# A selective scan on one core: ScalarE's products redistributed over a chunk, the product delta*x behind the matrix work, sums first in their place, finish and gate drawn out

## The chip, the cores and the metric

The kernel runs on one core of a Trainium2 chip. A core has five engines that run side by side, each with its own instruction stream: TensorE (PE in the profile, with its weight loads PEld), VectorE (DVE), ScalarE (ACT), GpSimd (POOL) and SyncE (SP, which here only issues DMAs). They wait for one another through semaphores. The metric is the time of one execution on the device, in microseconds (us); the kernel before takes 30205.28 us, the median of 3 runs (30204.43 to 30206.26).

## What is computed

Two layers work on an image of 256 x 256 tokens with 128 channels, all in float32. The first is row-wise attention with a pair bias and a gate. The second is a block with a two-dimensional selective scan: a projection to 256 inner channels, a depthwise 3x3 convolution and silu, then four scans (rows and columns, forwards and backwards), whose outputs are added, normalised, gated and projected back. The change touches only the scan stage. Its core in the reference:

```
delta = jax.nn.softplus(dts + dt_bias[None, :, :, None])
def step(h, inp):
    d_t, x_t, B_t, C_t = inp
    dA = jnp.exp(d_t[..., None] * As)
    h = dA * h + (d_t * x_t)[..., None] * B_t[:, :, None, :]
    y = jnp.einsum('bkdn,bkn->bkd', h, C_t)
    return (h, y)
```

So each of 256 channels has 16 states n. Per token the state is multiplied by exp(-delta*A), delta*x*B is added, and the output is the sum over n of h*C. After the four directions: y is normalised over its 256 channels, multiplied by the gate z = silu(...), multiplied by `w_out`, and added to the layer's input.

## The kernel before

The scan stage takes the last 24.5 ms of the span. It goes through 512 **chunks** q of 512 tokens: directions k in the order 2, 1, 3, 0, with 128 chunks each. A chunk has eight **steps** g, one for each group of 32 channels; on the 128 partitions lie 32 channels times 4 sets of states, and each partition holds 4 states i. A step has four places n = 0 to 3. I number the places of a chunk t = 4g + n, from 0 to 31; a number with a prime (1') is a place of the next chunk.

All instructions of the stage are recorded in the order of the program text (`manual_schedule`), so each engine executes exactly in the order in which the loop at L1140 to L1200 names its work. In every step:

- ACT makes four decays exp(delta*A): two go to the PSUM tile `dA`, of which there is one (places 0 and 1, L1109), and two to `dAl` in SBUF, two buffers, for the step after (places 2 and 3).
- DVE runs a scan of 512 on state 2 at place 0 and on state 3 at place 1 (L1176), each reading a `dAl` and a PSUM tile `bl`; at place 2 the product `bx<-B_r,ur` for the next step (L892, in `begin`); at place 3 one scan of 1024 over states 0 and 1 together, which reads `dA` (L1193).
- PE turns products back into `bl` (`turn_back`, L867) right after each short scan, and spreads delta*x over the partitions into the only `ur` tile (`spread_du`, L882) at place 2.
- POOL adds the carried state to the next step's first column (L1125), saves the last column times `a0x` (L1197), and multiplies the whole `bx` tile by C (L1200).

`bx` has 7 buffers: the product at place 2 of step g=6 writes the buffer that step g=0 of the same chunk had, and the one of g=2 the buffer of g=4 of the chunk before.

Around the steps, generators supply one piece of their work at each place, a piece ending at a `yield`; `until(a, b)` yields b - a times and so puts empty places in:

- `prepare(q+2)` readies a chunk two ahead: PE turns the tokens (`tps`), ACT copies them (`xs`, L752), PE projects (`pb`), ACT copies (`bc`), PE makes `pv`, ACT computes delta by Softplus (L776) and stores it by DMA; POOL multiplies delta*x (L781); PE turns `bc` and `xs` (`tpb`, `tpd`), ACT copies (`B_t` L790, `duT` L825). For the carry between chunks POOL forms `a0x` = A*delta of the first token (L813) and ACT takes its Exp (L821). The PSUM tag "mm" has 2 buffers for all these tiles.
- `products(q+1)` has 32 products duT*B on ACT (`bt`, L855), one a piece.
- `sums(q, h)` adds h*C over the states with PE, 16 matmuls in 4 pieces (`yp`, L906), half a chunk each.
- `store` (the first three directions) adds the partial output of an earlier direction to the new one on PE (`tpy`), ACT copies it (`yt`), a DMA stores it. `finish` (the last direction) adds in the same way (`ysum`), then normalises: ACT copies `ys` (L981), DVE takes statistics (L989, L991), POOL forms the inverse root (L36 to L994), ACT applies it (L997), PE turns (`tpz`), ACT scales (`gz`, L1021), POOL multiplies by the gate (L1025), PE projects (`po`, L1034), ACT copies (`xo`, L1044).

Within a place the order is: the place's decay, the pieces in a fixed order (`later`, which holds store and finish; preparing; replicating; multiplying; summing), then the scan or product of the place with its `turn_back` or `spread_du`.

Of the kernel before, what the change touches and what calls it, by code (L numbers as in the profile page):

```python
# [11 lines left out]
ALU = mybir.AluOpType  # L12
# [54 lines left out]
def attention_and_scan_kernel(  # L67
# [27 lines left out]
    nc = tc.nc  # L95
# [635 lines left out]
    def until(now, then):  # L731

        for _ in range(then - now):
            yield

    def prepare(q):

        k, a = steps[q]
        xt = loaded.pop(q)
        xs = io.tile([P, 2, T], F32, name="xs", bufs=3)  # L740
        tps = []
        for h in range(2):
            tp = sps.tile([P, T], F32, name="tps", tag="mm")
            for j in range(4):
                nc.tensor.transpose(  # L745
                    tp[:, j * P : (j + 1) * P], xt[:, j, h * P : (h + 1) * P], ident
                )
            tps.append(tp)
            yield
        yield from until(2, 4)  # L750
        for h, tp in enumerate(tps):
            nc.scalar.copy(xs[:, h, ::-1] if k >= 2 else xs[:, h, :], tp)  # L752
            yield
        yield from until(6, 7)
        pb = sps.tile([R + 2 * NS, T], F32, name="pb", tag="mm")
        for h in range(2):
            nc.tensor.matmul(
                pb, xw_in[:, k, h, :], xs[:, h, :], start=(h == 0), stop=(h == 1)
            )
        yield from until(7, 10)  # L760
        bc = io.tile([R + 2 * NS, T], F32, name="bc", bufs=1)
        nc.scalar.copy(bc, pb)
        bc_d = sd.tile([2 * NS, T], F32, name="bc_d")
        nc.sync.dma_start(bc_d, bc[R:, :])
        yield from until(10, 12)
        delta = io.tile([P, 2, T], F32, name="delta", tag="xd", bufs=1)
        pvs = []
        for h in range(2):
            pv = sps.tile([P, T], F32, name="pv", tag="mm")
            nc.tensor.matmul(  # L770
                pv, dtw_s[:, k, h * P : (h + 1) * P], bc[:R, :], start=True, stop=True
            )
            pvs.append(pv)
        yield from until(12, 15)
        for h, pv in enumerate(pvs):
            nc.scalar.activation(  # L776
                delta[:, h, :], pv, AF.Softplus, bias=dtb_s[:, k, h : h + 1]
            )
        de_d = sd.tile([DI, T], F32, name="de_d", bufs=3)
        nc.sync.dma_start(de_d.rearrange("(h p) t -> p h t", p=P), delta)  # L780
        nc.gpsimd.tensor_tensor(xs, delta, xs, ALU.mult)  # L781
        yield
        tp = sps.tile([P, 4, R + 2 * NS], F32, name="tpb", tag="mm")
        for b in range(4):
            nc.tensor.transpose(
                tp[:, b, :], bc[:, b * P : (b + 1) * P], ident[: R + 2 * NS, : R + 2 * NS]
            )
        yield from until(16, 18)
        B_t = io.tile([P, 4, R + 2 * NS], F32, name="B_t")
        nc.scalar.copy(B_t, tp)  # L790
        yield from until(18, 20)
        de0 = io.tile([P, NG, 1], F32, name="de0", bufs=1)
        if a:
            for j in range(4):
                nc.sync.dma_start(
                    de0[32 * j : 32 * j + 32],
                    de_d.rearrange("(g c) t -> c g t", c=32)[:, :, 0:1],
                )
        yield from until(20, 24)
        tps = []  # L800
        for w in range(2):
            tp = sps.tile([P, 2, DI], F32, name="tpd", tag="mm")
            for b in range(2):
                for h in range(2):
                    t0 = (2 * w + b) * P
                    nc.tensor.transpose(
                        tp[:, b, h * P : (h + 1) * P], xs[:, h, t0 : t0 + P], ident
                    )
            tps.append(tp)
            yield  # L810
        first = a0x[:, q % 2, :, :NB]
        if a:
            nc.gpsimd.tensor_tensor(  # L813
                first,
                A_s[:, k, :, :, :NB].rearrange("p h q i -> p (h q) i"),
                de0.to_broadcast([P, NG, NB]),
                ALU.mult,
            )
        yield from until(26, 28)
        if a:  # L820
            nc.scalar.activation(first, first, AF.Exp)  # L821
        duT = io.tile([P, 4, DI], F32, name="duT")
        prepared[q] = xs, de_d, duT, bc_d, B_t
        for w, tp in enumerate(tps):
            nc.scalar.copy(duT[:, 2 * w : 2 * w + 2, :], tp)  # L825
            yield
# [89 lines left out]
    def load_sum(q):  # L916

        k, a = steps[q]
        yl = io.tile([P, 4, DI], F32, name="yl", bufs=1)
        src = tokens(y_d[([K, *ORDER])[ORDER.index(k)]], k, a)  # L920
        n = 4 // len(src)
        for w, s in enumerate(src):
            nc.sync.dma_start(yl[:, n * w : n * w + n, :], s)
        return yl
# [33 lines left out]
    def finish(q, yos):  # L958
# [20 lines left out]
        ys = io.tile([P, 4, DI], F32, name="ys", tag="yt", bufs=1)  # L979
        for g, ps in enumerate(sums_):  # L980
            nc.scalar.copy(ys[:, 2 * g : 2 * g + 2, :], ps)  # L981
            if g == 0:
                yield
        st = io.tile([P, 4, 6], F32, name="yst")
        mv = io.tile([P, 4, 2], F32, name="ymv")
        rs = io.tile([P, 4], F32, name="yrs")
# [5 lines left out]
        rsqrt(nc, rs, mv[:, :, 1], 1e-5, neg_half)  # L992
        nc.gpsimd.tensor_tensor(nb, mv[:, :, 0], rs, ALU.mult)
        nc.gpsimd.tensor_scalar(nb, nb, -1.0, None, ALU.mult)  # L994
        yield from until(6, 8)
        for j in range(4):
            nc.scalar.activation(  # L997
                ys[:, j, :],
# [5 lines left out]
            if j == 1:  # L1004
                yield
                zt = io.tile([P, 2, T], F32, name="zl", tag="yl", bufs=1)
                nc.sync.dma_start(zt, z_d[:, a : a + T].rearrange("(h p) t -> p h t", p=P))
        yield from until(9, 11)
        tps = []
        for h in range(2):  # L1010
            tp = sps.tile([P, T], F32, name="tpz", tag="mm")
# [3 lines left out]
                )  # L1015
            tps.append(tp)
            yield
        yield from until(13, 15)
        gz = io.tile([P, 2, T], F32, name="gz", tag="yt", bufs=1)
        for h, tp in enumerate(tps):  # L1020
            nc.scalar.activation(  # L1021
# [10 lines left out]
        for j in range(4):  # L1032
            for h in range(2):
# [5 lines left out]
                    stop=True,  # L1039
                    skip_group_check=True,  # L1040
                )
        yield from until(23, 27)
        xo = io.tile([P, 4, D], F32, name="xo", tag="xr", bufs=1)
        nc.scalar.copy(xo, po)  # L1044
        nc.sync.dma_start(out[a : a + T, :].rearrange("(j p) c -> p j c", p=P), xo)
# [1 line left out]
    NQ = len(steps)  # L1047
    all_steps = [(q, g) for q in range(NQ) for g in range(NG)]
    drs, urs, hcs, yps, yos = {}, {}, {}, {}, {}
    preparing, later, finishing = [], [], []  # L1050
# [70 lines left out]
    def begin(q, g):  # L1121
# [3 lines left out]
            nc.gpsimd.tensor_tensor(hs[:, :NB, 0], hs[:, :NB, 0], hst[:, g, :NB], ALU.add)  # L1125
        bxs[q, g] = hs

    bxs, dAls = {}, {}
    for i in range(NB, NI):
        long_decay(0, 0, i)  # L1130
# [3 lines left out]
    for s, (q, g) in enumerate(all_steps):  # L1134
# [5 lines left out]
        for n in range(4):  # L1140
            if n < NB:
                decay(dA[:, n, 1:], q, g, n, 1)
            elif nxt:
                long_decay(*nxt, n)
            if n == 1 and g == 0 and q + 1 < NQ:
                multiplying.append(products(q + 1))
            if n == 2 and g == 6 and q + 3 < NQ:
                load(q + 3)
            if n == 0 and g == 1 and q + 2 < NQ:
                preparing.append(prepare(q + 2))  # L1150
            if n == 2 and g == 2 and q + 1 < NQ:
                replicating.append(replicate(q + 1))
            if n == 3 and g == 0 and q:
                evacuate(q - 1, 0)
                begin_sums(q - 1, 1)
            if n == 1 and g == 3 and q:
                evacuate(q - 1, 1)
                begin_sums(q, 0)
            if n == 1 and g == 1 and q:
                summing.append(sums(q - 1, 1))  # L1160
            if n == 3 and g == 4:
                summing.append(sums(q, 0))
            if n == 1 and g == 5 and finishing:
                later.append(finishing.pop())
            if n == 2 and g == 3 and q:
                summed[q - 1] = load_sum(q - 1)
            pieces(later)
            piece(preparing)
            piece(replicating)
            piece(multiplying)  # L1170
            if n == 3 and g < 6:
                piece(multiplying)
            piece(summing)
            if n < NI - NB:
                i = NB + n
                nc.vector.tensor_tensor_scan(  # L1176
                    hs[:, i, :],
                    dAls.pop((q, g, i)),
                    bls.pop((q, g, n)),
                    0.0 if a == 0 else hst[:, g, i : i + 1],  # L1180
                    ALU.mult,
                    ALU.add,
                )
                if nxt:
                    bls[(*nxt, n)] = turn_back(*nxt, n)
            elif n == 2:
                if nxt:
                    begin(*nxt)
                if s + 2 < len(all_steps):
                    urs[all_steps[s + 2]] = spread_du(*all_steps[s + 2])  # L1190
            else:
                run = hs[:, :NB, :].rearrange("p i t -> p (i t)")
                nc.vector.tensor_tensor_scan(  # L1193
                    run, dA.rearrange("p i t -> p (i t)"), run, 0.0, ALU.mult, ALU.add
                )
# [74 lines left out]
```

## Time and profile before

| What | Value |
|---|---|
| median of 3 runs | 30205.28 us |
| the profiled execution | 30277.23 us, its span 30275.4 us |
| mean granted TensorE clock | 0.901 |
| DVE busy, share of the span | 26766.9 us, 88% |
| PE busy | 25636.7 us, 85% |
| ACT busy | 24387.3 us, 81% |
| POOL busy | 23332.3 us, 77% |
| DVE busy from 12000 to 18000 us | 5809.76 of 6000 us |

The profile page has busy times, then groups of instructions by line with the mean duration of one instruction and the idle time of its engine before it. The stage changed here is the part from about 5.7 ms to the end. Starts that follow one another in the timeline may be closer together than a duration, since an instruction's end is recorded after the next has started.

In the last direction a chunk is longer than in the others: the copy `xo`, once a chunk, is recorded 106 times from 24518.3 to 29959.0 us, 51.8 us apart; the first three directions have the Exp of `a0x` 212 times from 12028.6 to 21977.2 us, 46.9 us apart (one chunk in it, the first of a direction, has none).

### The profile page before, as it was taken

The page shows a single profiled execution, that of the slowest core. Times are in us where ns is not written, and L with a number is a line of the kernel's source. Part 1 is how long each engine was busy: PE and PEld are TensorE (multiplying, and loading weights), DVE is VectorE, ACT ScalarE, POOL GpSimd, SP SyncE. Part 2 cuts the span into 40 slices and gives each one's busy share as a digit, 9 for nine tenths or more (in the row PEclk, how much of TensorE's full clock was granted, in tenths as well). Part 3 has the DMA queues.
Part 4 walks back from the last instruction along what each step waited for, and adds up shares of the span by engine and source line. Part 5 has one row for each costly group of instructions (what it writes and reads, how often), then busy time and mean ns, then how long its engine had stood idle before and what let it go on. Part 6 is the DMA issues. An engine that isn't in the chain of part 4 may idle for free. (4 is left out here: it accounts for less than half of the span.)

```text
span 30275.4 us, 414158 instructions
## 1 busy us (share of the span) xinstructions
PE 25636.7 (85%) x140314; PEld 12605.4 (42%) x140314; DVE 26766.9 (88%) x24930; ACT 24387.3 (81%) x47871; POOL 23332.3 (77%) x14327
## 2 busy tenths in 40 slices
PE   6999989888888888888888888888888888888887
PEld 2555545433333333333333333333333444444444
DVE  8666643699999999999999999999999999999998
ACT  5555532688888888888888888888888888888888
POOL 4222222688888888888888888888888888888888
PEclk9999999888888888888888888888888899999998
DMA  4001025455444544554555445545555444444444
GB/s 152 27 29 30 28 90 177 137 125 125 125 125 125 126 125 126 125 125 125 125 125 126 125 126 126 125 125 125 125 125 125 124 123 124 123 123 124 123 124 115
DMA packets 2737778, 3522.72 MB, mean 116 GB/s; under 512 B 707225, under 2 KB 1824281, under 8 KB 2659745
## 3 DMA queue, kind: packets, MB, share of 16 engines
q1 hardware_dynamic: 2730480, 3478.11, 44.6%
q8 instruction: 1105, 18.10, 0.3%
q10 hardware_dynamic: 5168, 18.12, 0.2%
q14 instruction: 1025, 8.39, 0.1%
HBM read 2689.15 MB, written 806.35 MB: 115 GB/s over the span
## 5 line engine op out<-in xcount | busy, mean ns | idle before, releaser
L1200 POOL TENSOR_TENSOR bx<-bx,C_r 128x2048 f32<-128x2048 f32 x4096 | 18654.0, 4554 | 337.5 <-DVE bx L1193 18.3
L1193 DVE TENSOR_TENSOR_SCAN bx<-dA,bx 128x1024 f32<-128x1024 f32 x4096 | 9362.9, 2286 | 661.9 <-ACT dA L1109 656.8
L1176 DVE TENSOR_TENSOR_SCAN bx<-dAl,hst,bl 128x512 f32<-128x512 f32 x8128 | 9876.0, 1258 | 1.5 <-ACT xs L752 0.4
L867 PE MATMUL bl<-ident,bt 128*128 128x128 f32 x32768 | 5805.2, 313 | 2781.2 <-DVE bx L1176 2724.7
L855 ACT ACTIVATE bt<-duT,B_t 128x256 f32<-128x256 f32 x16384 | 7930.0, 504 | 0.0
L1109 ACT ACTIVATE dA<-dr,A_s 128x511 f32<-128x511 f32 x8192 | 5607.4, 685 | 2677.6 <-DVE bx L1193 2569.8
L867 PEld LDWEIGHTS bl<-ident,bt 128*128 128x128 f32 x32768 | 4021.9, 156 | 6384.4 <-DVE bx L1176 5105.9
L1109 ACT ACTIVATE dAl<-dr,A_s 128x512 f32<-128x512 f32 x8192 | 5859.7, 715 | 109.5 <-DVE bx L1176 109.5
L882 PE MATMUL ur<-xs,spread 128*128 128x512 f32 x8192 | 5418.5, 748 | 554.6 <-DVE bx L892 550.6
L892 DVE TENSOR_TENSOR bx<-B_r,ur 128x1024 f32<-128x1024 f32 x4096 | 4926.1, 1203 | 387.9 <-PE yp L906 264.0
L906 PE MATMUL yp<-bx,gather 128*32 128x512 f32 x32768 | 4657.4, 652 | 1.2 <-ACT yo L1075 1.2
L370 POOL TENSOR_TENSOR at<-at,sm 128x2048 f32<-128x2048 f32 x256 | 922.7, 3604 | 2716.0 <-DVE sm L369 2716.0
L882 PEld LDWEIGHTS ur<-xs,spread 128*128 128x128 f32 x8192 | 1436.7, 220 | 2075.9 <-DVE bx L892 1215.6
L1197 POOL TENSOR_TENSOR hst<-bx,a0x 128x4 f32<-128x4 f32 x4064 | 823.7, 203 | 1619.0 <-DVE bx L1193 1608.0
L781 POOL TENSOR_TENSOR xs<-delta,xs 128x1024 f32<-128x1024 f32 x512 | 1214.1, 2371 | 824.1 <-ACT delta L776 824.1
L906 PEld LDWEIGHTS yp<-bx,gather 128*32 128x32 f32 x32768 | 733.4, 113 | 1804.4 <-issue 1119.3
L362 ACT ACTIVATE at<-at,mx 128x256 f32<-128x256 f32 x2048 | 1019.4, 502 | 473.5 <-DVE mx L358 468.8
L770 PE MATMUL pv<-bc,dtw_s 8*128 8x512 f32 x2048 | 1071.0, 632 | 63.5 <-ACT xo L1044 62.2
L745 PE MATMUL tps<-ident,xtok 128*128 128x128 f32 x4096 | 792.5, 328 | 309.5 <-ACT gz L1021 285.7
L389 ACT COPY aT<-atp 128x512 f32<-128x512 f32 x512 | 300.3, 586 | 917.2 <-PE atp L382 578.5
L391 DVE COPY aT<-atp 128x512 f32<-128x512 f32 x512 | 353.8, 691 | 771.9 <-PE atp L382 761.4
L745 PEld LDWEIGHTS tps<-ident,xtok 128*128 128x128 f32 x4096 | 640.8, 177 | 879.7 <-ACT gz L1021 441.3
(168 smaller groups left out, 28219.9 us busy)
## 6 DMA issues: line engine op xcount, KB each, us to landing
dr<-de_d SPq DMA_DIRECT2D x4096, 256.0 KB
C_r<-bc_d SPq DMA_DIRECT2D x2048, 256.0 KB
de_d<-delta SPq DMA_DIRECT2D x512, 512.0 KB
B_r<-bc_d SPq DMA_DIRECT2D x2048, 128.0 KB
xtok<-xc_d SPq DMA_DIRECT2D x256, 512.0 KB
yl<-y_d SPq DMA_DIRECT2D x256, 512.0 KB
xtok<-xc_d SPq DMA_DIRECT2D x512, 256.0 KB
yl<-y_d SPq DMA_DIRECT2D x512, 256.0 KB
```

Of the source, the lines that this page charges most:

```text
L745: nc.tensor.transpose(tp[:, j * P : (j + 1) * P], xt[:, j, h * P : (h + 1) * P], ident)
L770: nc.tensor.matmul(pv, dtw_s[:, k, h * P : (h + 1) * P], bc[:R, :], start=True, stop=True)
L781: nc.gpsimd.tensor_tensor(xs, delta, xs, ALU.mult)
L855: nc.scalar.mul(bt[:, b, :, j, :], duT[:, b, :].rearrange("t (g c) -> t g c", c=32), B_t[:, b, n : n + 1],)
L867: nc.tensor.transpose(bl[:, b * P : (b + 1) * P], bt[:, b, g].rearrange("t j c -> t (j c)"), ident)
L882: nc.tensor.matmul(ur, spread[:, g % 4].rearrange("p j c -> p (j c)"), prepared[q][0][:, g // 4, :], start=True, stop=True,)
L892: nc.vector.tensor_tensor(bx[:, :NB, :], replicas[q][0], ur.unsqueeze(1).to_broadcast([P, NB, T]), ALU.mult,)
L906: nc.tensor.matmul(yp[32 * g : 32 * g + 32, :], gather, hc[:, i, :], start=(i == 0), stop=True, skip_group_check=True,)
L1109: nc.scalar.activation(to, drs[q, g][:, t0:], AF.Exp, scale=A_s[:, steps[q][0], g // 4, g % 4, i : i + 1],)
L1176: nc.vector.tensor_tensor_scan(hs[:, i, :], dAls.pop((q, g, i)), bls.pop((q, g, n)), 0.0 if a == 0 else hst[:, g, i : i + 1], ALU.mult, AL ...
L1193: nc.vector.tensor_tensor_scan(run, dA.rearrange("p i t -> p (i t)"), run, 0.0, ALU.mult, ALU.add)
L1200: nc.gpsimd.tensor_tensor(hs, hs, replicas[q][1], ALU.mult)
```

## The change

The order of the work changes, no arithmetic and no tile.

- `prepare(q+2)` is added at place 5 and no longer at place 4, and its empty places are made fewer. The Softplus pieces go from place 19 to place 18, POOL's delta*x from place 19 to place 20 (behind the turning of `bc`), `tpd` from places 28 and 29 to 26 and 27, POOL's `a0x` from 30 to 28, the Exp of `a0x` and the two copies `duT` from 0' and 1' to 29 and 30.
- The products: none at places 0 and 17 to 20; two at n = 3 and at places 22 and 26; one at the others. They are given out until all 32 are done, the last at place 28 (before: place 26).
- `sums` is first among the pieces of a place and no longer last. It starts at place 4 (before 5) for the chunk before's second half, and at place 20 (before 19) for the first half.
- `store` and `finish` start at place 20 (before 21). In `finish` a place lies between the second copy `ys` and the statistics; ScalarE's scaling `gz` comes at places 3' and 4' (before 4' and 5'), `po` at 11' (before 12'), `xo` at 14' (before 16').

```
+    SHARE = [0 if t in (0, 17, 18, 19, 20) else 1 + (t % 4 == 3 or t in (22, 26)) for t in range(32)]
...
-            if n == 0 and g == 1 and q + 2 < NQ:
+            if n == 1 and g == 1 and q + 2 < NQ:
                 preparing.append(prepare(q + 2))
...
-            if n == 1 and g == 1 and q:
+            if n == 0 and g == 1 and q:
                 summing.append(sums(q - 1, 1))
-            if n == 3 and g == 4:
+            if n == 0 and g == 5:
                 summing.append(sums(q, 0))
-            if n == 1 and g == 5 and finishing:
+            if n == 0 and g == 5 and finishing:
                 later.append(finishing.pop())
...
+            piece(summing)
             pieces(later)
             piece(preparing)
             piece(replicating)
-            piece(multiplying)
-            if n == 3 and g < 6:
+            for _ in range(SHARE[4 * g + n]):
                 piece(multiplying)
-            piece(summing)
```

In `prepare`:

```
-        yield from until(2, 4)
+        yield from until(2, 3)
         for h, tp in enumerate(tps):
             nc.scalar.copy(xs[:, h, ::-1] if k >= 2 else xs[:, h, :], tp)
             yield
-        yield from until(6, 7)
...
-        yield from until(7, 10)
+        yield from until(5, 8)
...
-        yield from until(10, 12)
+        yield from until(8, 10)
...
-        yield from until(12, 15)
+        yield from until(10, 13)
...
-        nc.gpsimd.tensor_tensor(xs, delta, xs, ALU.mult)
         yield
...
-        yield from until(16, 18)
+        yield
+        nc.gpsimd.tensor_tensor(xs, delta, xs, ALU.mult)
+        yield
...
-        yield from until(18, 20)
+        yield from until(16, 18)
...
-        yield from until(20, 24)
+        yield from until(18, 21)
...
-        yield from until(26, 28)
+        yield
         if a:
             nc.scalar.activation(first, first, AF.Exp)
```

In `finish`:

```
-            if g == 0:
-                yield
+            yield
...
-        yield from until(6, 8)
+        yield from until(7, 9)
...
-        yield from until(9, 11)
+        yield from until(10, 12)
...
-        yield from until(13, 15)
+        yield from until(14, 15)
...
-        yield from until(23, 27)
+        yield from until(23, 26)
```

## Prediction

> **What bounds the kernel now.** I read the page first, then the waits of DVE for the three storing directions and for the last one apart, then the timeline around Softplus. On the page, three groups of the scan stage:
>
> ```profile
> L1200 POOL TENSOR_TENSOR bx<-bx,C_r 128x2048 f32<-128x2048 f32 x4096 | 18654.0, 4554 | 337.5 <-DVE bx L1193 18.3
> L1193 DVE TENSOR_TENSOR_SCAN bx<-dA,bx 128x1024 f32<-128x1024 f32 x4096 | 9362.9, 2286 | 661.9 <-ACT dA L1109 656.8
> ...
> L892 DVE TENSOR_TENSOR bx<-B_r,ur 128x1024 f32<-128x1024 f32 x4096 | 4926.1, 1203 | 387.9 <-PE yp L906 264.0
> ```
>
> DVE works almost without a break (5809.76 us of 6000), so its few waits are all there is to win. The waits view, 5700 to 23600 us (381 chunks of 46.93 us): engine and line that waited, releaser, us in total, times, longest.
>
> ```profile
> DVE bx L1193 <- ACT dA L1109: 445.9, 379, 1.3
> DVE bx L892 <- PE ur L882: 80.8, 189, 0.6
> DVE bx L892 <- PE yp L906: 34.6, 95, 0.4
> ```
>
> That is one wait of 1.18 us a chunk for `dA` and 0.30 us on PE: 1.48 us. The same view from 23600 us (128 chunks of 51.8 us):
>
> ```profile
> DVE bx L892 <- PE yp L906: 229.4, 126, 2.7
> DVE bx L1193 <- ACT dA L1109: 208.3, 126, 1.7
> DVE yst L989 <- ACT ys L981: 135.4, 250, 0.7
> ```
>
> Here it is 1.8 + 1.65 + 1.06 = 4.5 us a chunk. Were every wait gone, 384 x 1.48 + 128 x 4.5 = 1144 us would be saved; that is the limit. The timeline of ACT shows where the 1.18 us arise (start, duration in us):
>
> ```profile
> 12007.14 0.71 ACT L1109 ACTIVATE dAl<-dr,A_s 128x512 f32<-128x512 f32 x1
> 12007.87 1.28 ACT L776 ACT_TABLE_LOAD   x1
> 12009.17 1.27 ACT L776 ACTIVATE delta<-pv,dtb_s 128x512 f32<-128x512 f32 x2
> 12010.32 0.90 ACT L855 ACTIVATE bt<-duT,B_t 128x256 f32<-128x256 f32 x2
> 12011.24 1.28 ACT L1109 ACT_TABLE_LOAD   x1
> 12012.53 0.69 ACT L1109 ACTIVATE dA<-dr,A_s 128x511 f32<-128x511 f32 x1
> ```
>
> Two table loads and two Softplus stand in one piece before the decays of g=5; the long scan that needs them starts at 12014.34, 1.18 us late. A step without a wait takes 5.66 us (short scans at 12003.96 and 12009.62). From its first short scan S0, the second (S1) is due at 1.17, the product B at 2.34, the long scan L at 3.46.
>
> **What the Trainium skill says.** "ScalarE: Activation LUTs", What ACT_TABLE_LOAD costs: about 1283 ns, plus about 1380 ns of draining. The trace has the 1.28 us, but the load starts 0.02 us after the instruction before it ends: I take 1.30 a load. "Perfetto Trace Analysis", Tensor Engine Instruction: ACT, DVE and GPSIMD are strict FIFO. The trace agrees: POOL idles 1.42 us for delta with a ready `bx` behind it. "TensorE: Matmul & The Clock Gate", Part 1: the array runs at half rate after too little activity, judged in windows of about 3.4 us. This trace has it twice a chunk, in stretches of 3.4 or 6.8 us; the windows view shows one (PE clock third from the end):
>
> ```profile
> 12006.70:12010.10 3.40, 3.22 (x10) 0.98 (x12) 3.40 (x3) 3.37 (x6) 2.39 (x2) 0.50 0.25 84
> ```
>
> **Softplus, moved ahead of the last `dAl` (storing chunk).** With S0 of g=4 at 0, ACT starts `dA` at 0.13, product 0.76, `dA` 1.15, `dAl` 1.77 to 2.48, load to 3.78, Softplus 3.80 to 5.06, load to 6.36, `dAl` to 7.08, then `dA` 6.98 and 7.59 to 8.27 (starts overlap by 0.1, as above). L of g=5 is due at 9.12: its 1.18 us are gone. But the last `dAl` feeds S1 of g=5, due at 6.83: 7.08 + 0.11 (the release, 12014.23 to 12014.34) is 0.36 late. In a finishing chunk g=3 has also `xo` (0.48), its ACT work is 5.9 us instead of 5.4 in 5.66, so g=4 begins 0.23 later: 0.6.
>
> **Products.** 32 as before. By start-to-start times (product 0.40, decay 0.61, copy 0.48) ACT's sum a step stays within 5.9 us; the last one, place 28, is ready a step before its `turn_back` is read. No cost; without that cover each would cost 0.40.
>
> **`duT` and the Exp of `a0x`, drawn into g=7: a new wait.** This is the edit that decides. Now the end of g=6 and of g=7 look so, POOL first, then ACT:
>
> ```profile
> 12023.01 4.53 POOL L1200 TENSOR_TENSOR bx<-bx,C_r 128x2048 f32<-128x2048 f32 x1
> 12027.50 0.22 POOL L813 TENSOR_TENSOR a0x<-A_s,de 128x16 f32<-128x16 f32 x1
> ```
>
> ```profile
> 12027.97 0.69 ACT L1109 ACTIVATE dA<-dr,A_s 128x511 f32<-128x511 f32 x1 [2.59 <-DVE bx L1193]
> 12028.60 0.20 ACT L821 ACTIVATE a0x<-a0x 128x16 f32<-128x16 f32 x1
> 12028.70 0.56 ACT L825 COPY duT<-tpd 128x512 f32<-128x512 f32 x1
> ```
>
> POOL's `a0x` goes from place 30 to 28, but in POOL's order still stands behind L1200 of g=6, which cannot start before L of g=6 ends: 0.45 after S0 of g=7 at best (12033.50 to 12033.95). So `a0x` ends at 0.45 + 4.55 + 0.18 = 5.18. The Exp moves three places up, in front of both `dAl` of g=7. ACT reaches it about 2 us after S0 and stands until 5.2. Then Exp 0.10, `duT` 0.47, `dAl` 0.71, release 0.11 and semaphore 0.1: the next chunk's S0 at 6.67 instead of 5.66, 1.0 us late, in all but 4 chunks. What queues behind the Exp are exactly those decays, and DVE waits for them. In a finishing chunk two normalisations (2 x 0.49) and a `duT` (0.46) follow before the second `dAl`: counted from the Exp it is released at 0.10 + 0.47 + 0.61 + 2 x 0.49 + 0.46 + 0.83 = 3.45, S1 would be due at 1.40 + 1.17 = 2.57: another 0.88.
>
> **delta*x on POOL.** Before L1200 of g=4 it idled POOL; behind it, POOL runs 6.1 to 10.68, delta*x (2.38) to 13.02, and L1200 of g=5 and 6 start at 13.4 and 18.35, against 17.8 on time. `a0x` is up to 0.53 later, unless DVE has been held up as long before. Readers of `xs` (`tpd`, place 26) and the `xtok` load on SP's queue behind it (slot free at 13.02, place 26 at 13.8) are not held up.
>
> **Sums and B of g=7.** B at place 26 writes the buffer of g=0, so it needs the last sums. These go from place 22 to 23 and so behind `spread_du` of place 22, which PE executes after `tpy`. Durations from a chunk at 11840 us: sums 1.0, four turns 0.5, `tpy` 1.85, `spread_du` 0.96, double at half clock. PE is clear at 5.65 after S0 of g=4, `tpb` 0.4, then four sums, two `turn_back`, `tpy`, `spread_du`: 7.86, and about 0.6 for half clock that ends at 7.3: 14.5. B is due at 11.32 + 0.36 + 2.34 = 14.03: 0.5 late. At full clock PE would be done by 13.9 (no wait); a half clock until 8.9 makes it 1.2. I take 0.9 in storing chunks, 0.6 in finishing ones (B is due 0.24 later there). Against now: 0.2, since DVE's 1.18 us covered it. The other place, B of g=3, gains: last sums at 7 instead of 8, ready at 13.6 against 13.7 due: 0.
>
> **Finish.** `gz` a place earlier and sums ahead of `tps`: the 1.8 us at B of g=3 go. The statistics have a place more, but the second `ysum` stands behind the last sums: done 2.0 after B is released, copy 0.7, against 1.12 + 0.70 after B: 0.75 stays of 1.06.
>
> **Sum.** Storing chunk: -1.48 + 0.36 + 1.0 + 0.9 = +0.78, x 384 = +300 us. Finishing chunk: -4.5 + 0.6 + 1.0 + 0.88 + 0.75 + 0.6 = -0.67, x 128 = -86 us. Net +214 on the profiled execution, 30275 to 30489. The median of the runs is 0.24% lower; there it is 30205 + 214, say 30415.
>
> **Rivals.** (1) The Exp does not hold ACT up, through an order I misread or a hold that decays ahead cover: storing -0.22 x 384 = -84, finishing -2.55 x 128 = -326: 29795, faster. For it: ACT has 2.59 us of idle time in g=7 now; against: the idle time lies after the `dAl`, the wait before them. It decides once the Exp costs S0 less than about 0.4. Chance 0.12. (2) PE stays at full clock in g=5: B waits for nothing, POOL's lateness leaves 1.53, storing +0.41 x 384 = 157, finishing -1.27 x 128 = -163: 30199, no change. For it: the half clock follows PE's activity, which shifts; against: every chunk has it now. Chance 0.18. (3) Half clock lasts longer or comes in more steps, B waits 1.7: +1.58 x 384 + 0.43 x 128: 30867. Chance 0.13. My own case, B waiting 0.5 to 1.3: 30265 to 30660, chance 0.57.
>
> The range 30110 to 30720 leaves out rival 1 and the upper half of rival 3. 0.2% (60 us) is about what a measurement here can tell from no change: faster 0.16 (rival 1 and a little of 2), same 0.12, slower 0.72.
>
> **What would show it.** In DVE's waits: the long scans on `dA` near 0; the short scans on `dAl`, about 0.36 us at g=5 and 1.0 at g=0, hence some 800 us in all; B (L892) on `yp` rather than `ur`, 0.5 to 1.2 us; `yst` on `ys` once a chunk. ACT's waits must show the Exp of `a0x` on POOL L813, some 3 us a chunk. Without that last row the prediction is wrong; with it and no DVE wait at S0 of g=0, my reading of the decays' lead is.

## The result and the profile after

The changed kernel takes 30520.42 us (median of 4 runs, 30517.34 to 30522.84), the kernel before 30204.85 us beside it (4 runs, 30198.63 to 30206.26). The ratio is 1.0105, with a 95% interval from 1.0087 to 1.0122: the change makes the kernel slower, by 316 us. The profiled execution of the changed kernel took 30521.15 us, its span 30519.4 us, and the mean granted TensorE clock went from 0.901 to 0.874.

The groups of the scan stage on the page, as for the kernel before (line, engine, operation; busy time and mean ns of one; idle time ahead of it and what ended it):

```profile
L1199 POOL TENSOR_TENSOR bx<-bx,C_r 128x2048 f32<-128x2048 f32 x4096 | 18641.5, 4551 | 344.6 <-DVE bx L1192 25.7
L1175 DVE TENSOR_TENSOR_SCAN bx<-dAl,hst,bl 128x512 f32<-128x512 f32 x8128 | 9954.5, 1258 | 662.2 <-ACT dAl L1108 636.2
L1192 DVE TENSOR_TENSOR_SCAN bx<-dA,bx 128x1024 f32<-128x1024 f32 x4096 | 9340.9, 2280 | 0.0
L892 DVE TENSOR_TENSOR bx<-B_r,ur 128x1024 f32<-128x1024 f32 x4096 | 4905.6, 1198 | 612.1 <-PE yp L906 573.6
```

None of these four became dearer; their durations are those of before within 0.5%. What changed is the last column. The short scans, not shown so far, had almost no idle time in the kernel before:

```profile
L1176 DVE TENSOR_TENSOR_SCAN bx<-dAl,hst,bl 128x512 f32<-128x512 f32 x8128 | 9876.0, 1258 | 1.5 <-ACT xs L752 0.4
```

The long scan's 661.9 us of idle time are gone. In their place the short scans have 662.2 us, nearly all behind `dAl`, and the product B has 612.1 us instead of 387.9. The waits of DVE by part of the run (total us, times, longest), first 5700 to 23600 us (375 storing chunks), then from 23600 us:

```profile
DVE bx L892 <- PE yp L906: 430.3, 375, 1.8
DVE bx L1175 <- ACT dAl L1108: 371.1, 747, 0.9
```

```profile
DVE bx L1175 <- ACT dAl L1108: 265.9, 391, 1.0
DVE bx L892 <- PE yp L906: 140.0, 90, 1.8
DVE yst L988 <- ACT ys L981: 85.1, 125, 0.7
```

From here on S0 and S1 are the two short scans of a step, and B is its product, named by the step g in which it is executed: B of g=6 and B of g=2 are what the prediction, going by the step that they serve, calls B of g=7 and B of g=3. A storing chunk waits 2.19 us where it waited 1.48: B of g=6 1.15, S0 of g=0 0.79, S1 of g=5 0.20 and 0.05 more at S1 of g=6. A finishing chunk waits 3.8 us where it waited 4.5. From the spacing of an instruction that comes once a chunk (the Exp of `a0x`, 12041.3 to 21981.4 us over 208 chunks; `xo`, 24516.8 to 30251.6 us over 112), a storing chunk went from 46.93 to 47.79 us and a finishing one from 51.82 to 51.20. That makes 384 x 0.86 - 128 x 0.62 = +251 us; the two spans differ by 244.

**Where S0's wait comes from.** The end of a storing chunk in the timeline (start, duration), POOL and then ACT:

```profile
15238.03 4.54 POOL L1199 TENSOR_TENSOR bx<-bx,C_r 128x2048 f32<-128x2048 f32 x1
15242.51 0.23 POOL L813 TENSOR_TENSOR a0x<-A_s,de 128x16 f32<-128x16 f32 x1
```

```profile
15242.77 0.22 ACT L821 ACTIVATE a0x<-a0x 128x16 f32<-128x16 f32 x1 [2.17 <-POOL a0x L813]
15242.90 0.57 ACT L825 COPY duT<-tpd 128x512 f32<-128x512 f32 x1
15243.36 0.72 ACT L1108 ACTIVATE dAl<-dr,A_s 128x512 f32<-128x512 f32 x1
```

ACT stands 2.17 us in front of a 0.22 us Exp, because POOL reaches the small product for `a0x` only after its 4.54 us product with C. The decay that S0 needs is two instructions behind the Exp, at 15243.36; S0 starts at 15244.12 instead of 15243.33:

```profile
15244.12 2.45 DVE L1175 TENSOR_TENSOR_SCAN bx<-dAl,hst,bl 128x512 f32<-128x512 f32 x2 [0.79 <-ACT dAl L1108]
```

Over the whole run ACT waits 1126.3 us in 508 chunks there, a row that the kernel before does not have.

**Where B's wait comes from.** The same chunk on PE, before B of g=6:

```profile
15225.39 1.83 PE L906 MATMUL yp<-bx,gather 128*32 128x512 f32 x8
...
15229.70 1.05 PE L930 MATMUL tpy<-ident,yo 128*128 128x128 f32 x8
...
15232.11 1.12 PE L882 MATMUL ur<-xs,spread 128*128 128x512 f32 x2
15233.17 1.06 PE L906 MATMUL yp<-bx,gather 128*32 128x512 f32 x8
```

```profile
15234.25 1.22 DVE L892 TENSOR_TENSOR bx<-B_r,ur 128x1024 f32<-128x1024 f32 x1 [0.99 <-PE yp L906]
```

Eight `yp` matmuls take 1.83 us at half clock and 1.06 at full. This is a chunk whose half clock lay from 15220.2 to 15226.9. From 15225.4 on PE works without a pause, and the last sums, which read the buffer that B overwrites, end 1 us too late. How long B waits depends on the half clock in that chunk. In three storing chunks that follow one another, counted from the chunk's first S0, it lay at 23.1 to 29.9 us, 23.6 to 30.4 and 20.4 to 30.7, and B waited 0.75, 0.99 and 1.68 us. Nearly all storing chunks are of one of these three kinds: of 381, 126 are of the first, 125 of the second and 125 of the third.

### The profile page after: what moved, and what is told of

Read it like the earlier page. It is cut to its first block, busy times and chain, and to the rows that moved or that the text cites. A ratio compares the mean times of both kernels' runs of the same rounds, so it can differ in the third digit from the quotient of the medians.

```text
span 30519.4 us, 412621 instructions
## 1 busy us (share of the span) xinstructions
PE 26498.1 (87%) x140314; PEld 12548.6 (41%) x140314; DVE 26834.1 (88%) x24930; ACT 24373.7 (80%) x47871; POOL 23318.0 (76%) x14327
## 5 line engine op out<-in xcount | busy, mean ns | idle before, releaser
L1175 DVE TENSOR_TENSOR_SCAN bx<-dAl,hst,bl 128x512 f32<-128x512 f32 x8128 | 9954.5, 1258 | 662.2 <-ACT dAl L1108 636.2
L867 PE MATMUL bl<-ident,bt 128*128 128x128 f32 x32768 | 5969.8, 317 | 2775.9 <-DVE bx L1175 2635.4
L855 ACT ACTIVATE bt<-duT,B_t 128x256 f32<-128x256 f32 x16384 | 7761.1, 498 | 0.0
L867 PEld LDWEIGHTS bl<-ident,bt 128*128 128x128 f32 x32768 | 4100.0, 158 | 6426.5 <-DVE bx L1175 5895.2
L882 PE MATMUL ur<-xs,spread 128*128 128x512 f32 x8192 | 5649.2, 778 | 409.8 <-DVE bx L892 400.7
L892 DVE TENSOR_TENSOR bx<-B_r,ur 128x1024 f32<-128x1024 f32 x4096 | 4905.6, 1198 | 612.1 <-PE yp L906 573.6
L906 PE MATMUL yp<-bx,gather 128*32 128x512 f32 x32768 | 4791.8, 660 | 1.7 <-ACT yo L1074 1.7
L769 PE MATMUL pv<-bc,dtw_s 8*128 8x512 f32 x2048 | 1300.2, 762 | 1.3 <-ACT bc L761 1.3
L951 ACT COPY yt<-tpy 128x512 f32<-128x512 f32 x768 | 446.2, 581 | 877.5 <-PE tpy L930 877.5
L821 ACT ACTIVATE a0x<-a0x 128x16 f32<-128x16 f32 x508 | 110.6, 218 | 1126.3 <-POOL a0x L813 1126.3
```

Source lines behind the costliest of these rows:

```text
L769: nc.tensor.matmul(pv, dtw_s[:, k, h * P : (h + 1) * P], bc[:R, :], start=True, stop=True)
L855: nc.scalar.mul(bt[:, b, :, j, :], duT[:, b, :].rearrange("t (g c) -> t g c", c=32), B_t[:, b, n : n + 1],)
L867: nc.tensor.transpose(bl[:, b * P : (b + 1) * P], bt[:, b, g].rearrange("t j c -> t (j c)"), ident)
L882: nc.tensor.matmul(ur, spread[:, g % 4].rearrange("p j c -> p (j c)"), prepared[q][0][:, g // 4, :], start=True, stop=True,)
L892: nc.vector.tensor_tensor(bx[:, :NB, :], replicas[q][0], ur.unsqueeze(1).to_broadcast([P, NB, T]), ALU.mult,)
L906: nc.tensor.matmul(yp[32 * g : 32 * g + 32, :], gather, hc[:, i, :], start=(i == 0), stop=True, skip_group_check=True,)
```

## The experiments

My theory: the Exp of `a0x`, moved in front of the last decays, costs S0 0.8 us in every chunk, and PE's crowded half-clock stretch costs B 1.15 us. The rivals: B's wait alone is enough and the Exp costs nothing further (or the other way round); the new place of the sums is itself to blame; the period of a chunk follows something else, such as the 3.4 us windows of the clock (47.79 us is close to 14 windows of 3.413 us, the length that the Trainium skill gives in "TensorE: Matmul & The Clock Gate", Part 1; the stretches of 6.8 and 10.2 us above are two and three of them).

The medians of all ten runs. Each ratio is to the kernel before on the same chip (30205 us for the changed kernel, 30231 to 30246 us for the experiments); the chunk columns are spacings in the traces, in us, those of the finishing chunks all from `xo`.

| Kernel | Median us | Ratio [95%] | Storing chunk | Finishing chunk | Clock |
|---|---|---|---|---|---|
| before | | 1 | 46.93 | 51.82 | 0.901 |
| after | 30520.42 | 1.0105 [1.0087, 1.0122] | 47.79 | 51.20 | 0.874 |
| e1: Exp late | 30116.28 | 0.9963 [0.9950, 0.9976] | 47.46 | 48.83 | 0.885 |
| e2: more work for PE | 30298.65 | 1.0021 [1.0013, 1.0029] | 47.22 | 51.19 | 0.932 |
| e3: sums from place 19 | 30521.00 | 1.0095 [1.0079, 1.0112] | 47.77 | 51.20 | 0.879 |
| e4: one more DVE copy | 30801.66 | 1.0188 [1.0172, 1.0203] | 48.04 | 52.50 | 0.884 |
| e5: e1 and e2 | 29480.83 | 0.9747 [0.9733, 0.9762] | 45.83 | 48.84 | 0.941 |
| e6: e1, `store` later | 29573.93 | 0.9779 [0.9764, 0.9794] | 46.07 | 48.84 | 0.895 |
| e7: before, Exp early | 30735.69 | 1.0164 [1.0147, 1.0181] | 47.77 | 52.99 | 0.883 |
| e8: `gz` back | 30530.91 | 1.0095 [1.0080, 1.0110] | 47.79 | 51.20 | 0.874 |
| e9: all cures | 29290.41 | 0.9688 [0.9672, 0.9704] | 45.59 | 48.05 | 0.974 |
| e10: e2, delta*x back | 30082.90 | 0.9950 [0.9935, 0.9965] | 46.64 | 51.19 | 0.938 |

**e1, the Exp of `a0x` back at 0'.** Only this is undone; POOL's `a0x` and the copies `duT` keep their new places.

```
-        if a:
-            nc.scalar.activation(first, first, AF.Exp)
...
         for w, tp in enumerate(tps):
             nc.scalar.copy(duT[:, 2 * w : 2 * w + 2, :], tp)
             yield
+        yield
+        if a:
+            nc.scalar.activation(first, first, AF.Exp)
```

> The changed kernel with one edit: ScalarE's Exp of a0x moved from place 29 to place 0' of the next chunk, behind both decays of g=7; the two copies duT stay at 29 and 30. If the Exp's wait for GpSimd is what holds DVE at the first short scan of a chunk (0.79 us in a storing chunk; 0.83 and 0.80 us in a finishing one), those waits go and nothing takes their place: storing chunk 47.78 - 0.79 to -0.95 us, finishing chunk 51.13 - 1.63, so about 500 to 560 us less, near 29990 us. Rival, the half-clock windows set the chunk: the period stays at 14 windows of 3.413 us (47.78) because the wait of B in g=6 grows by what is saved: within 100 us of 30520 in the storing part.

The kernel becomes faster than the one before. DVE's waits from 5700 to 23600 us:

```profile
DVE bx L893 <- PE yp L907: 583.7, 413, 1.8
DVE bx L1176 <- ACT dAl L1109: 76.0, 377, 0.4
```

S0's wait is gone, and in the last direction S1's with it: a finishing chunk loses 2.37 us, 0.7 more than I expected, part of it at B (0.7 instead of 1.1). A storing chunk loses only 0.33, less than I expected, since B of g=6 now waits 1.5 us instead of 1.15, and S1 of g=6 0.16. So S0's late start had covered part of PE's work: both waits hang on one another, and neither alone is the price of the change.

**e7, the early Exp alone in the kernel before.** `a0x` goes to place 28 on POOL and its Exp to place 29 on ACT, in front of the decays of g=7; all else is as before.

```
         yield from until(20, 24)
+        if a:
+            nc.gpsimd.tensor_tensor(
+                first,
+                A_s[:, k, :, :, :NB].rearrange("p h q i -> p (h q) i"),
+                de0.to_broadcast([P, NG, NB]),
+                ALU.mult,
+            )
...
         for w in range(2):
+            if a and w == 1:
+                nc.scalar.activation(first, first, AF.Exp)
             tp = sps.tile([P, 2, DI], F32, name="tpd", tag="mm")
```

> The kernel before, with one part of the change alone: GpSimd's a0x at place 28 and its Exp at place 29, in front of both decays of g=7; all else as before. If this placement alone costs what I say, DVE waits at each chunk's first short scan: a0x ends 5.5 us after the first scan of g=7 (27.72 - 22.20), Exp 0.2, decay 0.7, release 0.1: 6.5 against 5.65, 0.7 to 0.9 us in 508 chunks, and some 0.4 us more in the 128 finishing ones: 350 to 500 us slower than before. Rival, ScalarE has the 2.6 us of slack in g=7 that the trace of before shows, and the Exp's place costs nothing: within 60 us of before.

This one move makes the kernel before 490 us slower, more than the whole change. ACT's waits of this kernel, and the end of a chunk on ACT:

```profile
ACT a0x L811 <- POOL a0x L802: 1711.0, 505, 3.7
```

```profile
15238.90 0.22 ACT L811 ACTIVATE a0x<-a0x 128x16 f32<-128x16 f32 x1 [3.65 <-POOL a0x L802]
15239.02 1.32 ACT L1109 ACTIVATE dAl<-dr,A_s 128x512 f32<-128x512 f32 x2
```

S0 waits only 0.31 us, not the 0.7 to 0.9 that I expected: here no `duT` stands between the Exp and the decay, and in the changed kernel that copy puts the decay 0.46 us further back (15242.90 to 15243.36). Most of the rest of the 0.84 us per storing chunk appears at B of g=6 (0.44 in place of 0.2) and B of g=2 (0.20 in place of 0.1), while the 1.17 us at the long scan stays. That a later chunk start alone makes these grow was not taken apart further. A finishing chunk grows by 1.17 us.

**e2, more work for PE.** In all four directions the turns for g=3, 4 and 5 write `bl` two or three times with the same values.

```
-        for b in range(4):
+        for b in [*range(4)] * {3: 2, 4: 3, 5: 3}.get(g, 1):
```

> The changed kernel with more work on PE: the turns back into bl are repeated, twice for the step after g=2, three times for the steps after g=3 and g=4, writing the same values (0.5 us each at full clock, PE is idle there). If it is the half clock after these quiet steps that makes B of g=6 wait 1.15 us for the last sums, PE stays at full clock in g=5, the wait falls to 0 to 0.3 us and a storing chunk from 47.78 to about 46.9: some 300 to 400 us less, near 30150. Rival, the sheer amount of work in front of B (four sums, two turns, tpy, spread_du): the wait stays at 1.1 us or grows by the added work, 30520 or more.

PE does more and the kernel gets faster: the clock rises from 0.874 to 0.932. DVE's waits from 5700 to 23600 us:

```profile
DVE bx L1175 <- ACT dAl L1108: 549.8, 756, 1.3
DVE bx L892 <- PE yp L906: 52.5, 135, 0.5
```

B of g=6 waits 0.015 us instead of 1.15; the 52.5 us of the second row are at B of g=2. From 5 us before S0 of g=4 up to B no storing chunk has a half-clock window any more. So in storing chunks half clock makes the difference between B on time and B 1.15 us late. But S0 now waits 1.25 instead of 0.79: with DVE no longer held up at B, POOL has no time to catch up. A storing chunk gains 0.57 us of the 1.15, and the kernel less than I expected. In finishing chunks B still waits, from 23600 us:

```profile
DVE bx L892 <- PE yp L906: 130.0, 125, 1.2
```

That is 1.04 us a chunk, and here it is not half clock: none of the 122 finishing chunks looked at has a half-clock window from 5 us before S0 of g=4 up to B. In the changed kernel 40 of 122 finishing chunks had a half clock that ended about 6 us after S0 of g=4, and there B waited for nothing. The added turns are in the way themselves: in a finishing chunk PE also makes `po` at that time, and with the turns repeated it has no pause up to B (in one chunk, from 27121.3 to 27142.4 us, it is busy 21.10 of 21.10 us at a clock of 1.00). The rival of this run, the sheer amount of work, holds in the last direction.

**e3, the old start of the sums.** The first half begins at place 19 again, still first in a place.

```
-            if n == 0 and g == 5:
+            if n == 3 and g == 4:
                 summing.append(sums(q, 0))
```

> The changed kernel with sums(q, 0) begun at place 19 again, as before the change, instead of 20. My working: PE's work between the end of POOL's product of g=3 and B of g=6 is the same in sum (only tpb and the sums change order, and B then waits for spread_du behind them instead of the last sums): the wait of B goes from 1.15 to 0.9 to 1.15 us, the time stays within 100 us of 30520, DVE's releaser becomes ur. Rival, the one place by which the last sums were put later is the cause: the wait falls to 0.2 us as in the kernel before, a storing chunk by 0.9 us, near 30100 us.

The time does not move. B waits 0.70 us, now for `ur`, and S1 of g=6 waits 0.45 for `bl`. PE has the same work to do by then, and only what stands last in its queue changes. The place of the sums is not the cause. That leaves the amount of work in the half-clock stretch, which e6 tests.

**e8, `gz` back at 4'.** `until(14, 15)` becomes `until(14, 16)`; the sums stay first.

> The changed kernel with the scaling gz back at places 4' and 5' (and po, xo and what follows one place later). The wait of 1.8 us at B of g=2 in finishing chunks is gone with the change. If putting the sums first among the pieces is what removed it, it stays away: within 60 us of 30520. If the earlier gz removed it (PE's tps waits for the PSUM buffers that gz frees), it comes back with 1 us or more: 128 x 1 to 1.8 us, 130 to 230 us slower.

No wait returns at B of g=2. So it was not the earlier `gz` that removed the 1.8 us which finishing chunks lost there before. What is left is the new order on PE: the sums begin at place 4, first among the pieces, and the turning of the tokens at place 5, where it was 5 and 4. Which of these moves did it was not taken apart.

**e4, one copy more on DVE.** At place 0 of g=2 DVE copies 128x256 elements that nobody reads.

```
+    idle = sw.tile([P, 256], F32, name="idle")
...
+            if n == 0 and g == 2:
+                nc.vector.tensor_copy(idle, spread[:, 0:2].rearrange("p q j c -> p (q j c)"))
```

> The changed kernel with one more instruction on VectorE in every chunk, a copy of 128x256 in SBUF at place 0 of g=2 (0.2 to 0.3 us), whose result nothing reads. If the chunk's period is held at 14 half-clock windows (47.79 us), the wait of B in g=6 gives way by as much and a storing chunk stays at 47.78 us: the time changes by less than 40 us. Rival, nothing holds the period: every chunk is longer by the copy, 512 x 0.2 to 0.3 us = 100 to 150 us more.

A storing chunk grows by 0.25 us, and the copy takes 0.27. A period held by the clock's windows would have stayed at 47.79, so this rival falls. What the finishing chunks do is told in the last section.

**e5, both cures at once.** e1 together with e2's repeats, these in the storing chunks alone.

> Both cures at once on the changed kernel: the Exp of a0x at place 0' of the next chunk, and the turns into bl repeated before g=5 (in storing chunks alone). Alone they left, in a storing chunk, a wait at the first scan of 1.25 us (repeats) and one at B of g=6 of 1.51 us (late Exp). If these are two separate causes, both waits vanish together and 0.2 us at the second short scan of g=5 stays: storing chunk 45.6 + 0.2 to 0.5 = 45.8 to 46.1 us, that is 1.4 to 1.7 us less than with the late Exp alone: about 29470 to 29580 us. Rival, a hidden third limit of about 46.9 us a chunk (PE or POOL): 29900 us or more.

Together they do far more than the sum of their parts in the storing chunks (-0.33 and -0.57 alone, -1.96 together), which is what two waits that cover each other give. Of DVE's waits 0.13 us are left at B of g=2 and 0.2 at S1 of g=5.

**e6, less work in the stretch instead of a faster clock.** e1, with `store` started at place 22 in the storing chunks (before: 20).

```
-            if n == 0 and g == 5 and finishing:
+            if finishing and (n, g) == ((0, 5) if last else (2, 5)):
```

Here `last` stands for: this chunk and the one before it are of the last direction. `tpd` and what follows it start two places later (`until(18, 23)`).

> The changed kernel with the Exp late, and store begun at place 22 instead of 20 (tpd and what follows it two places later), so that tpy no longer stands among the sums in front of B of g=6; nothing is repeated on PE. If B waits for the amount of PE's work in front of it, half clock or not, then 1.85 us less of it (3.7 at half clock) takes the wait from 1.51 to 0 to 0.3 us: a storing chunk at 45.8 to 46.2 us, near 29500 to 29650 us. Rival, the half clock alone decides: the wait stays above 1 us, 30000 us or more.

The Exp of `a0x`, behind `tpd` in the same generator, thereby comes at 2' and no longer at 0'. `tpy` now stands behind the last sums. The mean clock is 0.895, below that of the kernel before, and still the storing chunks take 46.07 us; B of g=6 waits 0.11. In 284 of 381 storing chunks the half clock still lasts two or three windows and ends 8 to 10 us after S0 of g=4. So the half clock as such costs little; it costs where PE's queue holds what DVE needs next.

**e10, delta*x back at place 19,** in front of the product with C, on top of e2.

```
+        nc.gpsimd.tensor_tensor(xs, delta, xs, ALU.mult)
         yield
...
         yield
-        nc.gpsimd.tensor_tensor(xs, delta, xs, ALU.mult)
         yield
```

> The changed kernel with the repeated turns (whose storing chunk waits 1.25 us at its first scan, against 0.79 without the repeats) and POOL's delta*x back at place 19, in front of the product with C of g=4. If delta*x behind that product makes POOL late until g=6 and so a0x and its Exp, POOL is up to 0.5 us earlier: the wait at the first scan falls from 1.25 to about 0.8 us, 384 x 0.4 = 150 us less than the 30299 us with the repeats alone (its ratio to before from 1.0021 to about 0.997). Rival, the wait grew because everything behind B of g=6 came earlier than the Exp could: delta*x's place is indifferent, ratio 1.001 to 1.003.

A storing chunk gains 0.58 us, more than the 0.4 expected, and S0's wait falls from 1.25 to 0.79; B of g=2 waits 0.1 us less. This is the lateness of POOL that delta*x behind the product brings: with PE out of the way, it lands at S0.

**e9, everything.** e6 with repeated turns at g=0, 1, 3, 4 and 5 of storing chunks and at g=4 and 5 of finishing ones (`{0: 2, 1: 3, 3: 2, 4: 3, 5: 3}` and `{4: 2, 5: 2}`).

> The cures together: Exp late, store from place 22, and repeated turns also around g=7, g=0 and in finishing chunks. If nothing but the waits seen so far is left, a storing chunk is 45.65 to 45.85 us (0.2 us at the second short scan of g=5 remains) and a finishing one 48.0 to 48.9: ratio to before 0.969 to 0.975. Rival, the added work on PE in g=7 and g=0 or in finishing chunks delays the scans it should help: ratio above 0.975.

3.1% faster than the kernel before, and by the two ratios 4.1% faster than the changed one (0.9688 / 1.0105). PE from 12000 to 22000 us, in the windows view (busy time and count of PE, PEld, DVE, ACT and POOL; then the clock, third from the end), and DVE's waits from 5700 to 23600 us:

```profile
12000.00:22000.00 10000.00, 9135.23 (x56149) 5248.00 (x56148) 9953.97 (x7019) 9152.70 (x17327) 9142.80 (x5685) 0.98 0.49 129
```

```profile
DVE bx L1178 <- ACT dAl L1111: 83.2, 392, 0.4
DVE bx L895 <- PE yp L909: 1.9, 3, 1.2
```

The clock is 0.98 where it was 0.88 before and 0.86 after. DVE is busy 9953.97 of 10000 us; what is left is S1 of g=5, 0.2 us a chunk, and in the last direction S1 (0.44) and the statistics (0.6).

## Why the prediction was right, and where its terms were off

The direction and the reasons held. In the profiles the forecast was +214 us, the spans show +244. Step by step:

- **Softplus.** The long scans on `dA` wait for nothing. The timeline has the step as worked out: two loads of 1.28 us around Softplus, and the last `dAl` late:

```profile
15221.70 1.28 ACT L775 ACT_TABLE_LOAD   x1
...
15224.28 1.28 ACT L1108 ACT_TABLE_LOAD   x1
15225.57 0.72 ACT L1108 ACTIVATE dAl<-dr,A_s 128x512 f32<-128x512 f32 x1
```

  S1 of g=5 waits 0.20 us for it, forecast 0.36; finishing 0.44, forecast 0.6.
- **Exp of `a0x`.** S0 1.0 us late in all but 4 chunks: recorded 0.79 (finishing 0.83), and S1 in finishing chunks 0.80 for 0.88. About 0.09 us comes on top of each recorded wait, since successive DVE instructions overlap by as much (a scan that ends at 15240.02 is followed by a product that starts at 15239.93) and a wait ends that. ACT's idle time is 2.2 us a chunk, forecast some 3, and DVE's waits on `dAl` are 636 us in all, forecast some 800. e1 and e7 show the cause.
- **delta*x.** POOL's lateness is real (e10), and stays hidden as long as B holds DVE up, as the forecast had it.
- **B of g=6.** The mis-sized term: 0.9 forecast, 1.15 measured; in finishing chunks 0.6 forecast, 1.1 measured. The working gave 0.5 for a half clock that ends 7.3 us after S0 of g=4 and 1.2 for one that ends at 8.9; 0.9 was put between them and not worked out, so that it came near is in part luck. Where the half clock did end at 7.3, B waits 0.75: the last sums end at 14.78, worked out were 14.5. In the third kind of chunk it ends at 8.0 but begins 2.2 us before S0 of g=4, while PE makes `pv`; PE is clear at 7.26 in place of 5.65, and B waits 1.68. That early start was not in the working. In the last direction 90 of 128 chunks wait, with up to 1.8 us.
- **Finish.** The 1.8 us at B of g=2 went, as forecast, but not through the earlier `gz` (e8). At the statistics 0.66 us stay, forecast 0.75; the figures that the working names there, 2.0 + 0.7 - 1.12 - 0.70, make 0.88.
- **Sum.** Storing +0.86 (forecast +0.78), finishing -0.62 (-0.67). Recorded waits explain +0.71; the lost overlaps of one or two more waits a chunk bring the rest within 0.06.
- **Products** cost nothing that DVE's waits show. They were not undone by themselves.

The step that missed most is the last one, from the profile to the median. I took it that the kernel after would also show a profiled execution 72 us above its median. It did not: 30521.15 against 30520.42. Why the profiled execution of the kernel before lay so high is open (on the chips of the experiments its median was 30231 to 30246 us); it accounts for some 70 of the 105 us between forecast and median.

**The rivals.** Rival 2, PE at full clock in g=5, was built as e2: 30199 forecast, no change; ratio 1.0021 measured. Its terms, 1.53 at S0 and 0.36 at S1, were 1.25 and 0.21; its saving in finishing chunks did not come, since there the added turns made B wait at full clock. Rival 1, an Exp that costs nothing, was built as e1. The forecast of 29795 left out that B's wait grows when S0 is on time, and 30116.28 was measured. Rival 3's B of 1.7 us occurs in a third of the storing chunks, not in the mean.

Two things stay open. Kernels with different waits (after, e3, e7, e8) all have storing chunks of 47.77 to 47.79 us; e4 shows that the windows do not hold this period, but not whether they pull on it. And the half clock itself is not forecast by anything here: what activity PE must show to keep its full clock was not found.

## What to carry to other kernels

An instruction moved up in an in-order queue takes its wait with it: ask not only whether the engine has idle time there, but where the releaser stands in its own queue and what is queued behind the moved instruction. Idle time of an engine is no cover when it lies behind the instructions that others need, and two waits that cover each other have to be removed together. Where an engine's clock follows its activity, look at the work that stands ahead of the critical read in its queue: take work out of it, or keep the engine busy in the quiet steps before. The second helps only where the engine has room: where it has none, as PE in the finishing chunks of e2, the added work delays the read itself.

## What was not expected of the hardware

**More work made PE's part quicker.** The trace of e9 has 56149 PE matmuls between 12000 and 22000 us, that of the changed kernel 40194, and the kernel is 4% faster. The Trainium skill ("TensorE: Matmul & The Clock Gate", Part 1) puts the cost of ramping up at under 1% of a typical span. Here the half clock comes back in every chunk, and the measurement decides: the first three directions alone went from 46.07 us a chunk (e6) to 45.59 with the repeats, 1.0%, and in a kernel where the stretch meets the critical path (e1 to e5) from 47.46 to 45.83, 3.4%.

**A copy on DVE that waits for GpSimd.** In e4 the copy takes 0.27 us in a storing chunk, where POOL is idle at that moment, and 1.84, the median, in the last direction: of its 129 copies from 24000 us on, 126 take over 1 us, and each of these starts while POOL multiplies by the gate; the 3 short ones do not. A finishing chunk grows by 1.3 us. The timeline of POOL, then of DVE:

```profile
26463.28 2.36 POOL L1024 TENSOR_TENSOR gz<-gz,zl 128x1024 f32<-128x1024 f32 x1
```

```profile
26463.96 1.83 DVE L1147 COPY idle<-spread 128x256 f32<-128x256 f32 x1
26465.71 2.44 DVE L1178 TENSOR_TENSOR_SCAN bx<-dAl,hst,bl 128x512 f32<-128x512 f32 x2
```

The copy ends at 26465.79, 0.15 us after POOL's product does (26465.64); in all 126 it is 0.15 to 0.16 us. This agrees with the Trainium skill ("SBUF — State Buffer", SBUF: two separate sides): DVE and GpSimd share a pair of ports, which a DVE instruction needs in a two-port mode or with two inputs in SBUF, and which one of the two engines holds for a whole instruction. Which of the ports this copy used, no run shows. The scans and products of this kernel, each with an operand in PSUM, show nothing of it: 1.26 and 1.20 us, although POOL works through nine tenths of the time.
